# Order of the sums, the W_h product and the values in layer 3 of a graph network

## The chip, the cores and the metric

One core of one Trainium2 chip runs the whole program. The metric is device time in microseconds. Engines are TensorE (PE), VectorE (DVE), ScalarE (ACT), GpSimd (POOL) and SyncE (SP); each runs its own list of instructions, and semaphores tie them together.

## The reference

Four layers work on x (32 graphs of 512 nodes with 64 features) and one adjacency matrix; each adds its result to x. Layers 0 to 2 are a graph convolution, a two-step convolution and a graph attention. The change touches only layer 3, an attention network of 8 heads and an output layer of the same form:

```
def gat_layer(x, graph, W, b):
    h = x @ W
    s = jnp.einsum('bnd,bmd->bnm', h, h) * graph
    s = jnp.where(s == 0.0, NEG_INF, s)
    a = jax.nn.softmax(s, axis=2)
    return jnp.einsum('bnm,bmd->bnd', a, h) + b
heads = jax.vmap(lambda W, b: gat_layer(flow_x, graph, W, b))(Wh, bh)
...
x = jax.nn.leaky_relu(cat, negative_slope=0.01)
out = gat_layer(x, graph, W_out, b_out)
return jax.nn.leaky_relu(out, negative_slope=0.01)
```

## The kernel before

Layers 0 to 2 take the first 450 us or so and are not touched. Layer 3 works on units. A heads unit (class Heads) is two heads of one graph; an output unit (class Out) is the output layer of two graphs. There are 128 of the first and 16 of the second, 144 in all, mostly eight heads units to one output unit; the last eight units are all output units. A unit is a pair k = 0, 1 of attention matrices of 512 x 512, and is worked in four row blocks r of 128 rows (128 partitions x 2 x 512 columns).

One call of period(t) (line 737) issues work for several units in different stages: unit(lag) is the unit that is lag places behind. The engines' orders are written out by hand: what stands earlier in period(t) stands earlier in the queue of its engine, on all five engines. The stages of a unit, with the lag at which they are done:

- scores (L383): TensorE forms a row block's two score matrices in PSUM, each from 64 of the array's rows. Blocks 0 and 1 are made one period ahead (lag -1), blocks 2 and 3 at lag 0.
- maxima (L395): VectorE adds the mask, writes the negated scores to SBUF (p) and keeps each row's extreme. spread_out and spread_in (L402, L410): SyncE sends these to DRAM (top_row) and brings them back copied to all partitions (topb).
- shift (L416, L420), at lag 1: GpSimd subtracts topb from p, in the order of row blocks 0, 2, 1, 3. exps (L429): ScalarE exponentiates; for odd blocks into PSUM (e_ps), and join (L432) on VectorE adds the even block before it.
- totals (L450), at lag 2: TensorE multiplies with ones to sum over rows, into a PSUM tile tot_ps; ScalarE copies it (L456); two small transfers, one from SyncE's and one from ScalarE's queue, lay it out as parts (L461). recips (L467, L470): VectorE adds the parts and takes reciprocals; recips_out (L474) and, at lag 3, recips_in (L481) spread them by way of DRAM (recb).
- values (L438), at lag 2: TensorE multiplies the attention matrices with the features into av, the only tile of the pool ps_v. normalize (L487), at lag 3: VectorE multiplies av by recb, which frees av.
- y_pe (L568), y_act (L578) and y_dve (L586), at lag 4: the W_h product of heads units in PSUM, then the bias and the leaky relu into cat. L578 writes 0.01 (y + b); L586 reads y again and takes the maximum. An output unit does back (L670, L675) and back_dve (L678) in this place.
- product (L613): TensorE adds cat times W_out into gT_ps; the cat of a unit is needed in the period in which it is made or in the next.

PSUM is handed out by pools of tiles. ps_s has two tiles of two banks, taken in turn by score blocks and by the exponentials of odd blocks. ps_m has two tiles of one bank; tot_ps, the two y_ps, back_ps, gV_ps, hx_ps and the two g_ps take them in turn in the order in which they are issued, and each waits until its buffer's last reader is done.

At a period's end come smaller steps: the transposes hx_ps (L310) and gV_ps (L629), the products g_ps (L550), their copies on ScalarE (L562), and features (L509 to L528), which normalises a graph ahead of its use.

Of the kernel before, what the change touches and what calls it, by code (L numbers as in the profile page):

```python
# [22 lines left out]
def fast_form(  # L23
# [25 lines left out]
    nc = tc.nc  # L49
    B, N, F = x.shape  # L50
    C = N // P
# [643 lines left out]
    def any_zero():  # L695

        def across(src, rows, name):
            ps = ps_m.tile([P, P], F32, name=name, tag="m")
            n = src.shape[0]
            nc.tensor.transpose(ps[:rows, :n], src, ident[:n, :n])  # L700
            return ps[:rows, :n]

        own = tiny.tile([P, 1], F32, name="own")
        nc.vector.tensor_reduce(own, least, AX.X, OP.min)
        two = tiny.tile([1, 2], F32, name="two")
        nc.vector.tensor_reduce(two[:, 0:1], across(own, 1, "own_ps"), AX.X, OP.min)
        best = tiny.tile([B // 2, 2], F32, name="best")
        nc.vector.tensor_reduce(
            best,
            across(least_out, B // 2, "out_ps").rearrange("b (k f) -> b k f", k=2),  # L710
            AX.X, OP.max,
        )
        worst = tiny.tile([B // 2, 1], F32, name="worst")
        nc.vector.tensor_reduce(worst, best, AX.X, OP.min)
        nc.vector.tensor_reduce(
            two[:, 1:2], across(worst, 1, "worst_ps"), AX.X, OP.min
        )
        flag = tiny.tile([1, 1], F32, name="flag")
        nc.vector.tensor_reduce(flag, two, AX.X, OP.min)
        nc.vector.scalar_tensor_tensor(  # L720
            again, flag, 0.0, unsound, op0=OP.is_equal, op1=OP.max
        )
# [6 lines left out]
    def planned(units, products):  # L729

        class Nothing:
            def __getattr__(self, name):
                return lambda *args: None

        nothing = Nothing()

        def period(t):
            def unit(lag):
                return units[t - lag] if 0 <= t - lag < len(units) else nothing

            now, ahead = unit(0), unit(-1)
            for r in range(2, C):
                now.scores(r)
            unit(3).recips_in()
            unit(6).store()
            unit(4).bias()
            if t != 1:
                unit(1).shift(0, nc.gpsimd)
                unit(1).exps(0)
            unit(2).totals()  # L750
            unit(2).totals_out(1, nc.scalar)
            u, h = products.get(t - 1, (None, 0))
            if u and h == H - 1:
                u.keep_product()
            if t != 1:
                unit(1).shift(2, nc.gpsimd)
                unit(1).exps(2)
            for r in range(2, C):
                now.maxima(r)
            now.spread_out()  # L760
            unit(2).totals_out(0, nc.sync)
            now.spread_in()
            for r in range(2):
                ahead.scores(r)
            unit(4).y_pe()
            unit(4).y_act()
            unit(3).normalize()
            for r in range(2):
                ahead.maxima(r)
            if t == 1:  # L770
                for r in (0, 2, 1, 3):
                    unit(1).shift(r, nc.vector)
                    if r < 3:
                        unit(1).exps(r)
            unit(4).back()
            unit(4).y_dve()
            unit(4).back_dve()
            if t != 1:
                unit(1).shift(1, nc.gpsimd)
                unit(1).exps(1)  # L780
            for j in range(C):
                unit(2).values(j)
            u, h = products.get(t, (None, 0))
            if u:
                u.product(h)
            unit(2).recips()
            unit(2).recips_out()
            unit(1).join(1)
            if t != 1:
                unit(1).shift(3, nc.gpsimd)  # L790
            unit(1).exps(3)
            unit(5).back_pool()
            unit(-2).make_gs()
            unit(1).join(3)
            unit(-3).features(3)
            unit(-2).judge_product()
            unit(1).make_v()
            unit(-4).make_hx()
            unit(-2).make_g()
            for step in range(3):  # L800
                for lag, odd in ((step - 7, 0), (step - 11, 1)):
                    u = unit(lag)
                    if getattr(u, "i", None) == 0 and u.b % 2 == odd:
                        u.features(step)
            if t == len(units) + 1:
                any_zero()

        return period
# [1067 lines left out]
```

## Time and profile before

| | us |
|---|---|
| median of 3 runs (lowest to highest) | 2043.86 (2043.75 to 2046.07) |
| profiled execution, its time | 2045.32 |
| its span | 2043.5 |
| PE busy | 1980.7 (97%) |
| DVE busy | 1753.4 (86%) |
| POOL busy | 1445.8 (71%) |
| ACT busy | 1295.2 (63%) |
| PE busy between 560 and 1900 us | 1335.7 of 1340 |

The granted clock of TensorE is 0.989 over the span. A busy share is a mean over all four layers; in layer 3 alone TensorE has work in nearly every moment. A line of the timeline gives the start, the time until the end of the last instruction merged into it, the engine and the line of the kernel, and, in brackets, the idle time ahead of it and what released it. Matmuls overlap: the distance from one start to the next is a better measure than the length.

### The profile page before, as it was taken

The numbers are of one execution on the slowest core, as the hardware profiler recorded it, in microseconds if no ns is written. First come the engines' busy times: TensorE is split into PE (matmuls) and PEld (weight loads), VectorE is DVE, ScalarE is ACT, GpSimd is POOL, SyncE is SP. The second block draws the span as 40 slices with busy tenths as digits, with TensorE's granted clock in tenths as the row PEclk, the third lists the DMA queues.
The fourth block names the chain that finished last, engine by engine and source line by source line (L and its number), as shares of the span: only waits on it lengthen the run. The fifth ranks groups of instructions, "written<-read, shape, count | busy, mean of one in ns | idle before, by whom it ended". The sixth has DMA issues, their size and how long they took to land.

```text
span 2043.5 us, 32571 instructions
## 1 busy us (share of the span) xinstructions
PE 1980.7 (97%) x11038; PEld 811.0 (40%) x11038; DVE 1753.4 (86%) x4121; ACT 1295.2 (63%) x1960; POOL 1445.8 (71%) x834
## 2 busy tenths in 40 slices
PE   7999999997999999999999999999999999999995
PEld 4676676762333333333333333333333333333332
DVE  6699996768988899889898898888898898888984
ACT  3443443346677777777677777676676776766674
POOL 2000000006898989899999989898888988889996
PEclk9999999988999999999999999999999999999999
DMA  5000000002222323232332323333232323323233
GB/s 143 1 1 1 1 2 1 1 1 69 70 73 79 82 77 75 79 80 79 75 85 74 84 69 85 75 77 76 76 77 69 79 75 69 79 74 80 71 83 81
DMA packets 186464, 129.31 MB, mean 63 GB/s; under 512 B 125048, under 2 KB 130336, under 8 KB 186160
## 3 DMA queue, kind: packets, MB, share of 16 engines
q1 hardware_dynamic: 167056, 126.35, 23.9%
q10 hardware_dynamic: 18720, 0.59, 0.5%
q8 instruction: 89, 1.46, 0.3%
q14 instruction: 87, 0.71, 0.1%
q0 software_dynamic: 512, 0.20, 0.1%
HBM read 119.48 MB, written 5.37 MB: 61 GB/s over the span
## 4 chain that ended last, share of the span: by engine, by line
PE 57%; POOL 8%; DVE 4%; DMA 4%; ACT 2%; issue 2%; ACTq 0%; SPq 0%; POOLq 0%; DVEq 0%
PE s_ps L383 20%; PE av L438 19%; POOL p_att L416 6%; PE tot_ps L450 5%; PE y_ps L568 5%; PE gT_ps L613 4%; PE g_ps L550 3%; DMA topb<-top_row 2%; DVE p_att L395 2%; POOL p_att L420 2%; DVE p_att L432 1%; DMA top_row<-top 1%; PE hx_ps L310 1%; ACT e_ps L429 1%; DVE cat L586 1%
## 5 line engine op out<-in xcount | busy, mean ns | idle before, releaser
L416 POOL TENSOR_TENSOR p_att<-p_att,topb 128x1024 f32<-128x1024 f32 x429 | 1008.1, 2383 | 0.0
L395 DVE CUSTOM_DVE_ANT_0 p_att<-s_ps,flow_neg 128x512 f32<-128x512 f32 x1152 | 726.1, 686 | 91.2 <-PE s_ps L383 89.6
L383 PE MATMUL s_ps<-g,hx 64*128 64x512 f32 x2048 | 515.3, 613 | 16.6 <-DVE p_att L432 14.5
L420 POOL TENSOR_TENSOR p_att<-p_att,topb 128x512 f32<-128x512 f32 x286 | 360.5, 1282 | 170.5 <-DMA topb<-top_row 140.1
L429 ACT ACTIVATE p_att<-p_att 128x1024 f32<-128x1024 f32 x288 | 304.8, 1059 | 173.7 <-POOL p_att L420 91.1
L432 DVE TENSOR_TENSOR p_att<-e_ps,p_att 128x1024 f32<-128x1024 f32 x288 | 338.9, 1198 | 35.5 <-ACT e_ps L429 34.3
L429 ACT ACTIVATE e_ps<-p_att 128x1024 f32<-128x1024 f32 x288 | 293.1, 1029 | 88.1 <-POOL p_att L416 81.3
L383 PEld LDWEIGHTS s_ps<-g,hx 64*128 64x128 f32 x2048 | 174.8, 186 | 329.0 <-DVE top L395 173.8
L438 PE MATMUL av<-p_att,hd 128*64 128x512 f32 x1024 | 269.7, 605 | 0.0
L438 PE MATMUL av<-p_att,hn 128*64 128x512 f32 x1024 | 263.2, 592 | 0.0
L1090 POOL TENSOR_TENSOR x<-x,bias_b 128x512 f32<-128x512 f32 x16 | 20.3, 1274 | 280.3 <-DVE hn L863 280.3
L586 DVE SCALAR_TENSOR_TENSOR cat<-y_ps,bh,cat 128x512 f32<-128x512 f32 x256 | 180.1, 745 | 15.3 <-ACT cat L578 14.0
L562 ACT COPY g<-g_ps 128x512 f32<-128x512 f32 x128 | 131.8, 1138 | 81.1 <-PE g_ps L550 81.1
L578 ACT ACTIVATE cat<-y_ps,bh 128x512 f32<-128x512 f32 x256 | 161.4, 682 | 33.1 <-PE y_ps L568 32.2
L450 PE MATMUL tot_ps<-p_att,ones 128*32 128x512 f32 x1152 | 156.1, 607 | 4.0 <-DVE p_att L432 4.0
L568 PE MATMUL y_ps<-o_att,wh_sb 64*128 64x512 f32 x512 | 137.4, 594 | 0.0
L438 PEld LDWEIGHTS av<-p_att,hn 128*64 128x64 f32 x1024 | 73.7, 137 | 146.1 <-issue 146.1
L613 PE MATMUL gT_ps<-cat,wo_sb 128*64 128x512 f32 x512 | 131.6, 592 | 0.0
L438 PEld LDWEIGHTS av<-p_att,hd 128*64 128x64 f32 x1024 | 62.2, 136 | 165.4 <-issue 132.5
L1014 PE MATMUL acc<-v,s 64*128 64x65 f32 x2048 | 124.0, 280 | 0.7 <-DVE s L1000 0.4
L487 DVE TENSOR_TENSOR o_att<-av,recb 128x512 f32<-128x512 f32 x144 | 99.2, 689 | 29.4 <-DMA recb<-rec_row 26.8
L1014 PEld LDWEIGHTS acc<-v,s 64*128 64x128 f32 x2048 | 121.0, 194 | 5.9 <-DVE o L1030 1.2
(183 smaller groups left out, 2113.9 us busy)
## 6 DMA issues: line engine op xcount, KB each, us to landing
topb<-top_row SPq DMA_DIRECT2D x288, 256.0 KB
recb<-rec_row SPq DMA_DIRECT2D x288, 128.0 KB
out_dram<-y SPq DMA_DIRECT2D x32, 128.0 KB
x<-in_x_dram SPq DMA_DIRECT2D x3, 1024.0 KB
top_row<-top SPq DMA_DIRECT2D x144, 4.0 KB
parts<-tot SPq DMA_DIRECT2D x144, 4.0 KB
parts<-tot ACTq DMA_DIRECT2D x144, 4.0 KB
rec_row<-rec_flow SPq DMA_DIRECT2D x144, 4.0 KB
```

The costliest lines, as they stand in the source:

```text
L383: nc.tensor.matmul(ps[:, k], lhsT=x[halves(k), r * P : (r + 1) * P], rhs=g[halves(k), :], start=True, stop=True,)
L395: nc.vector.tensor_tensor_reduce(out=self.p[r][:, k], in0=ps[:, k], in1=flow_neg[:, r], scale=-1.0, scalar=BIG, op0=OP.add, op1=OP.min, ac ...
L416: engine.tensor_tensor(self.p[r], self.p[r], self.topb, OP.subtract)
L420: engine.tensor_tensor(p, p, self.topb[:, k], OP.subtract)
L429: nc.scalar.activation(to, self.p[r], AF.Exp, scale=-1.0)
L432: nc.vector.tensor_tensor(self.p[r], self.joined, self.p[r - 1], OP.add)
L438: nc.tensor.matmul(self.av[halves(k), :], lhsT=self.v(k, j) if j % 2 else self.less_next(k, j), rhs=self.p[j][:, k], start=(j == 0), stop= ...
L450: nc.tensor.matmul(ps[q : q + 32, :], lhsT=ones, rhs=self.p[2 * e + 1][:, k], start=True, stop=True,)
L568: nc.tensor.matmul(ps, lhsT=wh_sb[halves(k), 2 * self.i + k, :], rhs=self.o[halves(k), :], start=True, stop=True,)
L586: nc.vector.scalar_tensor_tensor(self.cat[:, k], self.y[k], bh[:, h : h + 1], self.cat[:, k], op0=OP.add, op1=OP.max,)
L613: nc.tensor.matmul(self.gps[halves(k), :], lhsT=wo_sb[:, h, :], rhs=Heads.cat.pop((self.b + k, h)), start=(h == 0), stop=(h == H - 1),)
L1014: nc.tensor.matmul(self.acc[k][:, r], lhsT=self.s[b // 2][halves(k), b % 2, r * P : (r + 1) * P], rhs=self.v[halves(k), b], start=(b == 0) ...
```

## The change

Only the order of the calls in period(t) changes. On TensorE the W_h product comes between score blocks 2, 3 and the next unit's blocks 0, 1, the sums come behind all four blocks, and the W_out product comes ahead of the values. On ScalarE the W_h product's bias follows the exponential of row block 2 and the copy of the sums follows it. On VectorE L586 comes straight after normalize and ahead of the next unit's maxima, and the reciprocals come between the two additions. On SyncE the transfer of the parts goes behind both topb transfers.

```
             if t != 1:
                 unit(1).shift(0, nc.gpsimd)
                 unit(1).exps(0)
-            unit(2).totals()
-            unit(2).totals_out(1, nc.scalar)
             u, h = products.get(t - 1, (None, 0))
             if u and h == H - 1:
                 u.keep_product()
             if t != 1:
                 unit(1).shift(2, nc.gpsimd)
                 unit(1).exps(2)
+            unit(4).y_pe()
+            unit(4).back()
+            unit(4).y_act()
             for r in range(2, C):
                 now.maxima(r)
             now.spread_out()
-            unit(2).totals_out(0, nc.sync)
             now.spread_in()
             for r in range(2):
                 ahead.scores(r)
-            unit(4).y_pe()
-            unit(4).y_act()
             unit(3).normalize()
+            unit(4).y_dve()
+            unit(4).back_dve()
+            unit(2).totals()
+            for e, queue in enumerate((nc.sync, nc.scalar)):
+                unit(2).totals_out(e, queue)
             for r in range(2):
                 ahead.maxima(r)
...
-            unit(4).back()
-            unit(4).y_dve()
-            unit(4).back_dve()
             if t != 1:
                 unit(1).shift(1, nc.gpsimd)
                 unit(1).exps(1)
-            for j in range(C):
-                unit(2).values(j)
             u, h = products.get(t, (None, 0))
             if u:
                 u.product(h)
+            for j in range(C):
+                unit(2).values(j)
+            unit(1).join(1)
             unit(2).recips()
             unit(2).recips_out()
-            unit(1).join(1)
```

More of the change, by code (lines that the diff above doesn't have):

```diff
@@ L749, in period @@
                 unit(1).exps(0)
-            unit(2).totals()
-            unit(2).totals_out(1, nc.scalar)
             u, h = products.get(t - 1, (None, 0))
@@ L757, in period @@
                 unit(1).exps(2)
+            unit(4).y_pe()
+            unit(4).back()
+            unit(4).y_act()
             for r in range(2, C):
@@ L760, in period @@
             now.spread_out()
-            unit(2).totals_out(0, nc.sync)
             now.spread_in()
@@ L764, in period @@
                 ahead.scores(r)
-            unit(4).y_pe()
-            unit(4).y_act()
             unit(3).normalize()
+            unit(4).y_dve()
+            unit(4).back_dve()
+            unit(2).totals()
+            for e, queue in enumerate((nc.sync, nc.scalar)):
+                unit(2).totals_out(e, queue)
             for r in range(2):
@@ L774, in period @@
                         unit(1).exps(r)
-            unit(4).back()
-            unit(4).y_dve()
-            unit(4).back_dve()
             if t != 1:
@@ L780, in period @@
                 unit(1).exps(1)
-            for j in range(C):
-                unit(2).values(j)
             u, h = products.get(t, (None, 0))
@@ L785, in period @@
                 u.product(h)
+            for j in range(C):
+                unit(2).values(j)
+            unit(1).join(1)
             unit(2).recips()
             unit(2).recips_out()
-            unit(1).join(1)
             if t != 1:
```

## The prediction

> **What bounds the kernel now.** I read the page's shares first, then the costliest groups, then the waits, then the timeline of single periods. A period is one call of period(t); S is the start of its first score block (score blocks 2 and 3 of unit t).
>
> ```profile
> PE 1980.7 (97%) x11038; PEld 811.0 (40%) x11038; DVE 1753.4 (86%) x4121; ACT 1295.2 (63%) x1960; POOL 1445.8 (71%) x834
> ...
> L416 POOL TENSOR_TENSOR p_att<-p_att,topb 128x1024 f32<-128x1024 f32 x429 | 1008.1, 2383 | 0.0
> ...
> L420 POOL TENSOR_TENSOR p_att<-p_att,topb 128x512 f32<-128x512 f32 x286 | 360.5, 1282 | 170.5 <-DMA topb<-top_row 140.1
> ```
>
> TensorE is 97% busy; in the middle of layer 3 (560 to 1900 us) it is busy 1335.7 of 1340 us. So any wait put ahead of a TensorE instruction costs its whole length. GpSimd subtracts the row minima (shift): two halves and three whole tiles, 2 x 1.28 + 3 x 2.38 = 9.7 us, and what it waits for is the topb transfer. The timeline of TensorE over one ordinary period:
>
> ```profile
> 1218.96 1.99 PE L383 MATMUL s_ps<-g,hx 64*128 64x512 f32 x8
> 1220.88 1.06 PE L450 MATMUL tot_ps<-p_att,ones 128*32 128x512 f32 x8
> 1221.88 1.99 PE L383 MATMUL s_ps<-g,hx 64*128 64x512 f32 x8
> 1223.70 1.02 PE L568 MATMUL y_ps<-o_att,wh_sb 64*128 64x512 f32 x4
> 1224.65 1.08 PE L438 MATMUL av<-p_att,gD 128*64 128x512 f32 x4
> ```
>
> The starts follow one another with hardly a hole: two score blocks 1.9, sums 1.0, two score blocks 1.8, W_h product (y) 0.95, values 3.5, W_out product 0.9, and what ends a period (g, hx or gV) 0.6 to 1.0. Nine periods (eight of heads, one of the output layer) take 1307.18 - 1210.16 = 97.0 us from sums to sums. The one with the output unit's transposes lasts 1251.05 - 1240.82 = 10.2, so one of heads lasts (97.0 - 10.2) / 8 = 10.85. The other engines in that period:
>
> ```profile
> 1218.22 2.50 POOL L420 TENSOR_TENSOR p_att<-p_att,topb 128x512 f32<-128x512 f32 x2 [1.80 <-DMA topb<-top_row]
> ...
> 1220.68 7.03 POOL L416 TENSOR_TENSOR p_att<-p_att,topb 128x1024 f32<-128x1024 f32 x3
> ...
> 1222.59 0.69 DVE L487 TENSOR_TENSOR o_att<-av,recb 128x512 f32<-128x512 f32 x1
> ...
> 1223.19 1.06 ACT L429 ACTIVATE p_att<-p_att 128x1024 f32<-128x1024 f32 x1 [0.59 <-POOL p_att L416]
> ...
> 1224.75 1.27 ACT L578 ACTIVATE cat<-y_ps,bh 128x512 f32<-128x512 f32 x2 [0.51 <-PE y_ps L568]
> ```
>
> The exponential of row block 2 starts at S + 4.2, when GpSimd's second shift is done; y is then copied and biased by ScalarE, and VectorE's maximum follows (L586, 0.75 each). None of this holds TensorE today: sums run at S + 1.9, before y exists.
>
> **The Trainium skill.** "PSUM — Partial Sum Buffer", section "Engine vs sequencer instructions", says that ScalarE, VectorE and GpSimdE queues are strict FIFO and that matmuls start and complete in program order. The traced order agrees: everything on an engine stands in the order of period(t). "DMA: Bandwidth & Descriptors", section "Anatomy of one DMA", gives about 2.0 us of fixed cost, mostly completion. Here SyncE waited 237.6 us in 144 cases for rec_row, 1.65 each, 1.97 with the 0.32 of issue. "Perfetto Trace Analysis", section "Optimization Strategy", says consistent bubbles on the engine that should be saturated can mean too few PSUM buffers; the trace before shows next to none at the sums (the L450 matmuls idled 4.0 us in the whole run).
>
> **The change part by part.**
>
> *TensorE order.* New: scores 2, 3; y; scores 0, 1 of the next unit; sums; W_out product; values. Scores and y have the same tile shape (64 x 128), so two shape changes around the sums go, and one (sums to W_out product) comes. From the start differences: scores to sums to scores cost 0.1 + 0.14 above 1.72 and 0.86, y to values 0.09. The new period with no wait is 5 x 0.86 + 0.1 = 4.4 before the sums, then 0.95 + 0.88 + 3.49 + 0.62 (mean of the endings) + 0.1 = 6.0: 10.4 to 10.5. That alone is 0.25 to 0.35 less than now.
>
> *A wait that comes in.* ps_m has two buffers. Before, the sums took them ahead of y0 and y1; now y0, y1 and then the sums take them in turn, so the sums need y0's buffer. Its last reader is the first L586 on VectorE. That stands behind L578 on ScalarE, which in the new order stands behind the exponential of row block 2, which waits for GpSimd's second shift. Measured from S at today's spacing, over ten periods from 1208 to 1315 us: the first shift starts 9.81 after the S of the period before; two halves and one whole tile, 4.81 from start to start, end at 14.62; +0.12 to the exponential, +0.96 until the next ScalarE instruction starts, 0.68 for L578, 0.03, 0.72 for L586, 0.1 to TensorE: the sums start at 17.23, which is S + 6.4 in today's 10.8. TensorE is there at S + 4.45. The stall is 2.0; the W_out product (which needs the second L586, 0.65 later) is then covered by the sums' 0.95, and values, the endings and the next period's scores all wait behind.
>
> *Feedback.* The shift follows scores of the period before, so a longer period brings it relatively earlier. Two periods = 17.23 + 6.0 = 23.2: 11.6 each. (Today's spacing would give 12.4; half the excess remains.)
>
> *The reciprocals' round.* Before, nothing led from normalize (L487) back to the sums. Now VectorE does L487 before L586 in the same queue, so a round of one period closes: sums to copy 1.13 and 0.59; the parts transfer, at most 3.2 by the rows (3.2 to 4.7 passed with no wait), but hidden, for the reduction stands behind the addition of row block 1, which needs its exponential after the copy and its 0.5 of DMA issue: 4.55 after the sums; reduction and reciprocal 0.35; rec_row 0.1 and 1.4 to 1.97 (1.4 where topb has landed, as it will have here); recb 3.6 (issue to L487 where it waited); L487 0.62, L586 0.72, 0.1: 11.45 to 12.0. It is about as long as the other round.
>
> *ScalarE in front of it.* In three of eight head periods (ScalarE's timeline: activations at 1232.07, 1253.09 and 1274.50 right after g's copies) the two copies (to S + 2.3) and the features' activations (1.06 to 1.26) come ahead of both exponentials: 2.3 + 1.1 + 2 x 0.96 + 0.68 + 0.75 + 0.1 = 6.75 for the sums, and 12.7 with 6.0 behind; since the next period can give some back, I take 12.3. Eight head periods: (5 x 11.6 + 3 x 12.3) / 8 = 11.86, 1.0 over today's 10.85. Some is lent back, so 0.95.
>
> *Queues.* SyncE issues the parts transfer after topb instead of before it: topb was waiting for top_row there anyway (131 us over 127 cases), so nothing is won; the parts come behind 512 KB of topb, hidden as above. ScalarE's parts issue moves with the copy. The output unit's transposes, one period in nine, hold no y buffer: no change. Join 1 ahead of the reciprocals costs nothing where the parts have landed, and it delays rec_row by 1.2, already counted. Layers 0 to 2 (to 450 us) are untouched.
>
> *Sum.* 128 head units x 0.95 = +122 us on the profiled span of 2043.5 (2045.3 with what lies around it; the median of the runs is 2043.9): 2165 us.
>
> **Rivals.** (a) The mean transfers are slower: rec_row at up to 4.0 and top_row at 3.0 as in their tails, with recb now later and so in front of top_row. The round is 12.2, +1.3 x 128 = 166: 2210. For it: both rounds are close, and the later of two counts every time. Against: topb no longer collides with rec_row. (b) Slow periods lend to fast ones and the output period resets the chain: nine periods are four pairs of 23.2 less shared endings and one of 10.2, some 102, +0.55 a period: 2115. (c) Other side: y's reader is in time and only the saved shape changes remain: -0.25 x 136 = -34, 2010. It would take L586 at S + 4.4, 1.9 us earlier than the table, so that GpSimd or ScalarE would have to run ahead of today; the 1.8 us that GpSimd waited for topb in the fenced line speak against slack there. (d) The buffers are not taken in turn and no wait arises; then (c) again or no change.
>
> **How the numbers follow.** Main case 0.5; (a) 0.22; (b) 0.17; (c) and (d) faster 0.08; unchanged 0.03. Slower 0.89. 0.2%, 4 us, is what a measurement can tell from no change. The range 2090 to 2225 leaves out the faster cases and the far end of (a); the main case alone is 2140 to 2190.
>
> **What would show it.** TensorE idle just before L450, some 1 to 2 us in head periods, released by VectorE's cat (L586); TensorE near 91%; the waits for topb on GpSimd grow; L487 waits for recb in most periods; L578 no longer waits for TensorE. Wrong if L450 has no idle time before it, if the stall stands at another line (values on L487, y on g's copy), or if head periods stay near 10.8.

## The result and the profile after

The changed kernel takes 2246.3 us in the median (2240.5 to 2250.5) against 2043.8 before: a ratio of 1.099, interval 1.095 to 1.102. It is slower, as forecast, but by 202.5 us where 121 were forecast, and it lies outside the range of 2090 to 2225.

The page after, shares and the groups that the prediction spoke of (in a group: busy time and mean of one, then the engine's idle time just before and what ended it):

```profile
PE 2020.9 (90%) x11038; PEld 846.0 (38%) x11038; DVE 1771.0 (79%) x4121; ACT 1290.2 (58%) x1960; POOL 1442.8 (64%) x834
...
L420 POOL TENSOR_TENSOR p_att<-p_att,topb 128x512 f32<-128x512 f32 x286 | 361.1, 1282 | 368.1 <-DMA topb<-top_row 321.7
...
L450 PE MATMUL tot_ps<-p_att,ones 128*32 128x512 f32 x1152 | 158.3, 622 | 145.5 <-DVE cat L586 144.4
...
L586 DVE SCALAR_TENSOR_TENSOR cat<-y_ps,bh,cat 128x512 f32<-128x512 f32 x256 | 179.7, 743 | 54.0 <-ACT cat L578 53.8
...
L487 DVE TENSOR_TENSOR o_att<-av,recb 128x512 f32<-128x512 f32 x144 | 99.4, 690 | 100.2 <-DMA recb<-rec_row 96.6
```

TensorE's busy time grows by 40 us and that of the others by less than 18. This growth is not more work, since the ends of matmuls are modelled: from the first to the last of the values' sixteen starts 3.04 us pass in the mean, 3.06 before. So the clock is not the cause either, though the one granted was 0.984 in this run and 0.989 before. The time is a new stall: TensorE stands ahead of the sums (L450) until VectorE's L586, where it hardly stood before. GpSimd's wait for topb grows from 140 to 322 us and L487's for recb from 27 to 97, both as announced. The chain that ended last, before the change 57% TensorE, is now this:

```profile
PE 26%; DMA 18%; ACT 14%; DVE 12%; issue 4%; POOL 2%; SPq 1%; ACTq 1%; DVEq 0%; POOLq 0%
```

One period of the timeline (start, us, engine, line; in brackets the idle time and its releaser):

```profile
1220.79 0.69 DVE L487 TENSOR_TENSOR o_att<-av,recb 128x512 f32<-128x512 f32 x1 [0.83 <-DMA recb<-rec_row]
1221.21 1.26 ACT L578 ACTIVATE cat<-y_ps,bh 128x512 f32<-128x512 f32 x2
...
1221.93 1.41 DVE L586 SCALAR_TENSOR_TENSOR cat<-y_ps,bh,cat 128x512 f32<-128x512 f32 x2 [0.45 <-ACT cat L578]
...
1222.74 1.07 PE L450 MATMUL tot_ps<-p_att,ones 128*32 128x512 f32 x8 [1.24 <-DVE cat L586]
1223.73 1.08 PE L613 MATMUL gT_ps<-cat,wo_sb 128*64 128x512 f32 x4
```

Here both late things meet at L586: recb held L487, and L578 then held L586 for 0.45 more. VectorE's waits for the two between 560 and 1900 us (us, times, longest; there are 110 periods):

```profile
DVE o_att L487 <- DMA recb<-rec_row: 66.6, 77, 2.2
DVE cat L586 <- ACT cat L578: 46.4, 41, 2.4
```

Taken period by period in this stretch of the trace, in 102 periods of heads only recb held VectorE ahead of the first L586 in 50, only L578 in 21, both in turn in 20, and neither in 11. The parts of a period, as means of the distances between starts in the timelines (560 to 1900 us, every unit): before, 1.96 from the first score block to the sums, 3.81 to the values, 5.02 to the next period's scores, 10.8 in all. After, 6.11, 1.95 and 4.19: 12.25. The period is 1.45 longer; 195.2 us of added span are 135 such periods.

### The profile page after: what moved, and what is told of

Read it like the earlier page. It is cut to its first block, busy times and chain, and to the rows that moved or that the text cites. A ratio compares the mean times of both kernels' runs of the same rounds, so it can differ in the third digit from the quotient of the medians.

```text
span 2238.7 us, 32504 instructions
## 1 busy us (share of the span) xinstructions
PE 2020.9 (90%) x11038; PEld 846.0 (38%) x11038; DVE 1771.0 (79%) x4121; ACT 1290.2 (58%) x1960; POOL 1442.8 (64%) x834
## 4 chain that ended last, share of the span: by engine, by line
PE 26%; DMA 18%; ACT 14%; DVE 12%; issue 4%; POOL 2%; SPq 1%; ACTq 1%; DVEq 0%; POOLq 0%
PE av L438 11%; DMA recb<-rec_row 8%; PE tot_ps L450 7%; DMA rec_row<-rec_flow 4%; ACT g L562 4%; DVE cat L586 4%; DMA parts<-tot 4%; PE gT_ps L613 3%; DVE p_att L395 3%; ACT p_att L429 3%; PE g_ps L550 2%; PE s_ps L383 2%; ACT e_ps L429 2%; DVE p_att L432 2%; DMA top_row<-top 2%
## 5 line engine op out<-in xcount | busy, mean ns | idle before, releaser
L395 DVE CUSTOM_DVE_ANT_0 p_att<-s_ps,flow_neg 128x512 f32<-128x512 f32 x1152 | 726.2, 685 | 113.5 <-PE s_ps L383 112.9
L383 PE MATMUL s_ps<-g,hx 64*128 64x512 f32 x2048 | 552.7, 610 | 21.8 <-DVE p_att L432 15.3
L432 DVE TENSOR_TENSOR p_att<-e_ps,p_att 128x1024 f32<-128x1024 f32 x288 | 345.2, 1199 | 59.4 <-ACT e_ps L429 59.2
L429 ACT ACTIVATE p_att<-p_att 128x1024 f32<-128x1024 f32 x288 | 297.8, 1054 | 91.1 <-POOL p_att L416 68.4
L429 ACT ACTIVATE e_ps<-p_att 128x1024 f32<-128x1024 f32 x288 | 285.2, 1020 | 99.0 <-DVE top L395 75.9
L383 PEld LDWEIGHTS s_ps<-g,hx 64*128 64x128 f32 x2048 | 205.5, 186 | 288.1 <-DVE top L395 114.3
L450 PE MATMUL tot_ps<-p_att,ones 128*32 128x512 f32 x1152 | 158.3, 622 | 145.5 <-DVE cat L586 144.4
L456 ACT COPY tot<-tot_ps 128x512 f32<-128x512 f32 x144 | 84.3, 585 | 265.2 <-PE tot_ps L450 265.2
L586 DVE SCALAR_TENSOR_TENSOR cat<-y_ps,bh,cat 128x512 f32<-128x512 f32 x256 | 179.7, 743 | 54.0 <-ACT cat L578 53.8
L487 DVE TENSOR_TENSOR o_att<-av,recb 128x512 f32<-128x512 f32 x144 | 99.4, 690 | 100.2 <-DMA recb<-rec_row 96.6
L568 PE MATMUL y_ps<-o_att,wh_sb 64*128 64x512 f32 x512 | 168.7, 599 | 0.0
L578 ACT ACTIVATE cat<-y_ps,bh 128x512 f32<-128x512 f32 x256 | 159.8, 676 | 4.5 <-PE y_ps L568 4.5
L613 PE MATMUL gT_ps<-cat,wo_sb 128*64 128x512 f32 x512 | 145.1, 647 | 0.0
L438 PEld LDWEIGHTS av<-p_att,hd 128*64 128x64 f32 x1024 | 74.0, 139 | 155.9 <-issue 144.6
```

Source lines behind the costliest of these rows:

```text
L383: nc.tensor.matmul(ps[:, k], lhsT=x[halves(k), r * P : (r + 1) * P], rhs=g[halves(k), :], start=True, stop=True,)
L395: nc.vector.tensor_tensor_reduce(out=self.p[r][:, k], in0=ps[:, k], in1=flow_neg[:, r], scale=-1.0, scalar=BIG, op0=OP.add, op1=OP.min, ac ...
L429: nc.scalar.activation(to, self.p[r], AF.Exp, scale=-1.0)
L432: nc.vector.tensor_tensor(self.p[r], self.joined, self.p[r - 1], OP.add)
L438: nc.tensor.matmul(self.av[halves(k), :], lhsT=self.v(k, j) if j % 2 else self.less_next(k, j), rhs=self.p[j][:, k], start=(j == 0), stop= ...
L450: nc.tensor.matmul(ps[q : q + 32, :], lhsT=ones, rhs=self.p[2 * e + 1][:, k], start=True, stop=True,)
```

## The experiments

The theory at the start: two rounds of dependencies meet at L586, the reciprocals' (sums, parts, rec_row, recb, L487, L586, sums) and GpSimd's (scores, topb, shift, exponential, L578, L586, sums). The rival: only one of them matters. For each kernel the mean period is given (distance from sums to sums between 560 and 1900 us, all units; where the stretch is cut moves it by up to 0.02); it is 10.80 before and 12.25 after.

**One round opened, then the other, then both.**

First, L578 goes ahead of the exponential on ScalarE:

```
-            if t != 1:
-                unit(1).shift(2, nc.gpsimd)
-                unit(1).exps(2)
             unit(4).y_pe()
             unit(4).back()
             unit(4).y_act()
+            if t != 1:
+                unit(1).shift(2, nc.gpsimd)
+                unit(1).exps(2)
```

> The changed kernel, with the W_h product's bias (L578) ahead of the exponential of row block 2 on ScalarE. Theory: two rounds meet at L586, and the reciprocals' round (sums, parts, rec_row, recb, normalize, L586, sums) of one period is the longer. Then only the lateness of L578 goes, 0.47 us between normalize and L586 in the mean of the changed kernel: 128 x 0.45 = 58 us off 2246, some 2190 us, with recb still waited for. Rival: GpSimd's shift by way of L578 sets the period and recb is only waited for because there is time: then this edit takes the stall away, 2010 to 2060 us.

Measured: 2203.5 us, ratio 1.078 (1.076 to 1.080), period 11.94. Only 43 us go, and VectorE still waits for recb (75.2 us in 76 cases between 560 and 1900), while L586 still waits for L578 in 24 cases (17.4 us). So the reciprocals' round holds the time nearly by itself.

Second, L586 goes ahead of normalize on VectorE:

```
-            unit(3).normalize()
             unit(4).y_dve()
             unit(4).back_dve()
+            unit(3).normalize()
```

> The changed kernel, with L586 (and the output unit's maximum) ahead of normalize on VectorE, so that nothing leads from recb to the sums. Theory: the period falls to that of GpSimd's round, 11.6 to 11.9 us for a heads unit against 12.35 now: 2150 to 2180 us, TensorE still idle ahead of L450, now behind L578. Rival (GpSimd's round alone set the period already): 2230 to 2250 us, as now.

Measured: 2194.3 us, ratio 1.073 (1.072 to 1.075), period 11.90. 52 us go, somewhat fewer than I expected. Among the waits of this kernel's VectorE between 560 and 1900 us hardly any is for recb any more; L586 waits for L578 instead:

```profile
DVE cat L586 <- ACT cat L578: 138.8, 92, 3.0
DVE p_att L395 <- PE s_ps L383: 61.3, 83, 2.4
DVE rec_flow L467 <- DMA parts<-tot: 35.0, 47, 1.8
DVE p_att L432 <- ACT e_ps L429: 6.1, 18, 0.7
...
DVE o_att L487 <- DMA recb<-rec_row: 1.8, 3, 0.9
```

The same round can be opened without touching any order, by taking away what makes L487 wait. This kernel multiplies by a tile that is ready and so leaves out the division by the sums:

```
-            nc.vector.tensor_tensor(self.o, self.av, self.recb, OP.mult)
+            nc.vector.tensor_tensor(self.o, self.av, urow, OP.mult)
```

> The changed kernel, where normalize multiplies by a tile that has lain ready since layer 2 (the node scales) instead of recb, so the division by the sums of the softmax is left out; all transfers are still issued, and L487 is as long as before and still ahead of L586. Theory: the reciprocals' round is open, GpSimd's round stays: 2170 to 2200 us, as with L586 ahead of normalize. Rival A (the round of the reciprocals alone made the time): below 2120 us. Rival B (recb was only waited for because there was time): 2235 to 2255 us.

Measured: 2196.6 us, ratio 1.073 (1.071 to 1.075), period 11.96; L586 waits for L578 for 83.6 us in 74 cases, and L487 for nothing. Two different edits, one on the queue and one on the transfer, give the same time. So GpSimd's and ScalarE's round is also a bound by itself, and nearly as long.

Third, both queue edits together:

> Both edits together: L578 ahead of the exponential, L586 ahead of normalize; TensorE's order is that of the changed kernel. Theory: neither round leads to the sums any more, the stall is at most what g's copies leave on ScalarE: 2000 to 2060 us, near the kernel before. Rival: the later sums make the reciprocals late all the same, or the buffer of y0 is late by TensorE's own order: over 2100 us.

Measured: 2110.0 us, ratio 1.032 (1.030 to 1.034), period 11.25. One edit gives 43, the other 52, both 136: as with two bounds of nearly one length, of which either holds what the other lets go. It misses my 2000 to 2060 and falls to the rival (over 2100): some 65 us of the loss belong to neither round. TensorE still stands 24.1 us ahead of the sums, in 41 cases between 560 and 1900.

**What is left without the rounds.** The next kernel adds to both edits that L578 stands ahead of both exponentials and of the copy of gT:

```
+            unit(4).y_pe()
+            unit(4).back()
+            unit(4).y_act()
             if t != 1:
                 unit(1).shift(0, nc.gpsimd)
                 unit(1).exps(0)
             u, h = products.get(t - 1, (None, 0))
...
-            unit(4).y_pe()
-            unit(4).back()
-            unit(4).y_act()
```

> As both edits together (L578 ahead of the exponential of block 2, L586 ahead of normalize, 2110 us), but L578 ahead of both exponentials and of the copy of gT on ScalarE. Theory: what was left of the stall at L450 (24 us between 560 and 1900) came from ScalarE's own work in front of L578 and shrinks by half or more, the rest of the gap to the kernel before is TensorE's order (scores to sums at least 4.82 us, no gain over the old order): 2085 to 2102 us. Rival: the first exponential, now later, delays the chain to the additions and takes it back: 2110 us or more.

Measured: 2093.2 us, ratio 1.024 (1.022 to 1.026), period 11.10. TensorE's waits between 560 and 1900 us no longer name the sums:

```profile
PE s_ps L383 <- DVE p_att L432: 14.5, 30, 1.3
PE gT_ps L613 <- ACT gT L621: 3.5, 8, 0.6
PE av L438 <- DVE o_att L487: 2.2, 3, 1.3
```

So the new order of TensorE, with no such stall at the sums, is still 0.30 longer per period than the old one. Its distance from scores to sums is 5.03 in the mean and never below 4.82. The chain that ended last in the kernel with both edits shows why, in order of time:

```profile
1229.39 1.08 PE s_ps L383 x4
1230.48 0.03 issue
1230.50 0.69 DVE p_att L395
...
1231.20 0.60 DVE p_att L395
...
1231.81 0.60 DVE p_att L395
...
1232.42 0.60 DVE p_att L395
...
1233.09 1.13 PE s_ps L383 x4
1234.22 1.00 PE tot_ps L450 x8
```

The next unit's second score block needs the buffer that VectorE reads last among four L395, so it starts 3.7 us after the period's start. Until then the new order gives TensorE four steps of 0.86 (two score blocks, the W_h product, the next unit's first block); the old order had the sums there too, and its second block started at 3.92. So VectorE sets the 4.82, where I had put TensorE's own 4.4. The list of waits does not name this hole: each block is shown with a modelled end 1.08 to 1.13 after its start, though the next can start 0.86 after it, and a hole as short as this is counted as busy. After a period that ends with g, the second y also waits for g's second copy: there the distance is 5.16 in the mean, otherwise 4.92.

**The sums alone.** In the kernel before, the sums move behind the next unit's two score blocks, with the copy and the parts; nothing else moves:

```
-            unit(2).totals()
-            unit(2).totals_out(1, nc.scalar)
...
-            unit(2).totals_out(0, nc.sync)
...
             for r in range(2):
                 ahead.scores(r)
+            unit(2).totals()
+            unit(2).totals_out(0, nc.sync)
+            unit(2).totals_out(1, nc.scalar)
             unit(4).y_pe()
```

> The kernel before, with only the sums (and their copy and the transfers of the parts) moved behind the next unit's two score blocks; the W_h product stays behind them, so the sums take their buffer ahead of y0 and wait for no L586. Theory: no stall at L450; recb comes about 0.5 us late for normalize, which holds VectorE, not TensorE: 2040 to 2085 us. Rival (late sums are what costs, through the reciprocals and not through the buffer): over 2150 us.

Measured: 2305.5 us, ratio 1.127 (1.125 to 1.129), period 12.64: far outside what I expected, and slower than the whole change. The number falls to the rival (over 2150), but its cause, the reciprocals, is not what the trace shows: between 560 and 1900 us L487 waits for recb only 5.5 us, in 11 cases. The timeline:

```profile
1223.07 2.26 PE L383 MATMUL s_ps<-g,hx 64*128 64x512 f32 x8 [0.65 <-DVE top L395]
...
1225.25 1.07 PE L450 MATMUL tot_ps<-p_att,ones 128*32 128x512 f32 x8
...
1226.25 1.90 PE L568 MATMUL y_ps<-o_att,wh_sb 64*128 64x512 f32 x4
1226.39 0.59 ACT L456 COPY tot<-tot_ps 128x512 f32<-128x512 f32 x1 [1.83 <-PE tot_ps L450]
...
1227.02 0.29 PEld L568 LDWEIGHTS y_ps<-o_att,wh_sb 64*128 64x128 f32 x2 [0.48 <-ACT tot L456]
...
1228.28 1.41 DVE L586 SCALAR_TENSOR_TENSOR cat<-y_ps,bh,cat 128x512 f32<-128x512 f32 x2 [1.10 <-ACT cat L578]
```

Two things that I had left out. The pool of two buffers ties in the other direction as well: with the sums next to the W_h product, the second y needs the buffer of the sums, and the pair of y takes 1.84 in the mean, from its start to that of the next tile, where it took 1.01. And the next unit's first block now waits 0.65 for VectorE, because the sums no longer fill the time before it: y starts 5.81 after the period's start, where it started at 4.79. These two, 0.83 and 1.02, are the whole of the 1.84 by which the period is longer. So this run doesn't tell the buffer from the place, as it was meant to; it shows that the old order had the two score blocks between the sums and y, which hid the sums' copy.

The hole ahead of the next unit's block was then measured alone, by moving one block ahead of the sums in the kernel before:

```
+            ahead.scores(0)
             unit(2).totals()
...
-            for r in range(2):
-                ahead.scores(r)
+            ahead.scores(1)
```

> The kernel before, with only one of the next unit's two score blocks moved ahead of the sums on TensorE: scores 2, 3, next 0, sums, next 1, W_h product. No buffer is taken in another order and the sums come one block later. Theory: next block 0 needs VectorE's maxima of block 2, which end at S + 2.4, so TensorE stands some 0.5 us that the sums used to fill: 144 x 0.5 = 72, 2095 to 2130 us. Rival: VectorE has slack and the sums' place among the blocks costs nothing, 2040 to 2055 us.

Measured: 2147.7 us, ratio 1.050 (1.048 to 1.052), period 11.56. TensorE waits for VectorE's maxima ahead of a score block:

```profile
PE s_ps L383 <- DVE top L395: 85.6, 141, 1.1
```

That is 0.6 in 141 of 144 units, as reckoned; with 102 us the loss is larger than these waits. The starts show the rest: the next unit's second block begins 4.65 after the period's start, where it began at 3.92, and this 0.73 is nearly all of the 0.76 by which the period is longer. The wait is counted from the modelled end of the block before and so falls short of the hole.

**The buffer.** The sums take the values' buffer in place of y0's; all orders stay those of the changed kernel:

```
-            ps = ps_m.tile([P, N], F32, name="tot_ps", tag="m")
+            ps = ps_v.tile([P, N], F32, name="tot_ps", tag="av")
...
-                self.av = ps_v.tile([P, N], F32, name="av")
+                self.av = ps_v.tile([P, N], F32, name="av", tag="av")
```

> The changed kernel with the sums in the values' PSUM buffer instead of the one of y0; all orders as in the changed kernel. Theory: the wait for y0's buffer is what ties the sums to L586; now they wait for normalize (L487), the last reader of the values, so recb still leads to them, but L586 and L578 no longer do, except where ScalarE's copy of the sums stands behind L578 and the values wait for that copy: the reciprocals' round is shorter by some 1.2 us, 2100 to 2165 us. Rival: the stall comes with the late place of the sums and not with the buffer: 2230 us or more.

Measured: 2191.0 us, ratio 1.071 (1.069 to 1.073), period 11.83. The sums' releaser changes to the last reader of the other buffer, as it must if the buffer is the tie:

```profile
PE tot_ps L450 <- DVE o_att L487: 50.5, 61, 2.6
```

The time falls by 55 us, not by the 81 to 146 that I expected: L487 waits for recb all the same (91.0 us in 87 cases). With L578 ahead of the exponential as well:

> The sums in the values' buffer, and L578 ahead of the exponential of row block 2. Theory: what was left through ScalarE's copy goes too, only normalize's wait for recb is in front of the sums: 2075 to 2115 us. Rival: no better than the buffer alone (within 10 us of it), because recb sets the period by itself.

Measured: 2165.3 us, ratio 1.059 (1.057 to 1.061), period 11.63. Here the reciprocals' round no longer passes through L586. Its pieces are: sums to copy 1.21, to the issue of the parts 0.75, to the reduction 3.12, to rec_row 0.43, to recb's issue 1.52, to L487 3.62, to the next sums 0.97; 11.62 in all. Pieces that lead from one sums to the next add up to the period whatever bounds it; that this round does so shows in its waits, of L487 for recb in 88 cases (84.1 us) and of the sums for L487 in 57 (48.4 us). The time lies 50 us above what I expected, and that of the kernel with the buffer alone 26 above: I had put this round too short.

**Two parts of the change undone in the changed kernel.** The reciprocals back ahead of both additions, and the W_out product back behind the values:

```
+            unit(2).recips()
+            unit(2).recips_out()
             unit(1).join(1)
-            unit(2).recips()
-            unit(2).recips_out()
```

> The changed kernel with the reciprocals back ahead of both additions on VectorE. Theory: the reciprocals' round sets the period in most heads units, and in it the reduction (L467) starts 2.95 us after the parts are issued, of which part is the addition of row block 1 in front; without it some 0.3 us of each round go: 2195 to 2220 us. Rival: the place of the reciprocals doesn't bear on the end, 2235 to 2255 us.

Measured: 2249.7 us, ratio 1.101 (1.098 to 1.104): no change to the kernel after. I had expected 25 us or more; the rival's value came. The trace shows that something did move: between 560 and 1900 us VectorE now stands 176.2 us for the parts, ahead of both additions (17.2 in the kernel after), and most of what TensorE wins at the sums (76.6 us of waiting against 116.6) it loses at the score blocks, which wait 37.9 us for the additions instead of 4.7.

```
-            u, h = products.get(t, (None, 0))
-            if u:
-                u.product(h)
             for j in range(C):
                 unit(2).values(j)
+            u, h = products.get(t, (None, 0))
+            if u:
+                u.product(h)
```

> The changed kernel with the W_out product back behind the values. Theory: its place neither costs nor saves, since L586 for the second head is over before the sums are: 2235 to 2255 us. Rival: it waits for cat in front of the values, and its old place gives 20 us or more back: below 2226 us.

Measured: 2242.9 us, ratio 1.096 (1.094 to 1.098): none either, as expected.

## Why the prediction was wrong

The sign, the place and the wait were right. The sum was too small, because it gave nothing to the meeting of the two rounds and put each of them somewhat too short. TensorE's new order, taken for a gain, is a loss; in the changed kernel the rounds are longer than that, and it shows only where they are opened.

*A wait that comes in* holds. L450's idle time, its releaser L586, the growth at topb and recb and TensorE at 90% are what it named. Where the buffer is changed, the releaser changes.

*TensorE order* failed. It put the period without a wait at 10.4 to 10.5, 0.25 to 0.35 less than before. (Against its own 10.85 for a unit of heads that would be 0.35 to 0.45 less.) Measured is 11.10, 0.30 more. I had added TensorE's blocks and left out that the next unit's score blocks need VectorE's four L395 of this period; the sums, a longer filler, had stood there. This also ends the rival (c): even without that stall at the sums the order is 48 us slower.

*Feedback* and *ScalarE in front of it* were too short. Their 11.86 for a heads unit is (8 x 11.86 + 10.2) / 9 = 11.68 over all units; the two kernels with the other round open measured 11.90 and 11.96. (The terms of the case with g's copies add up to 6.85, not 6.75; the 12.3 taken for it does not rest on that.) The entry of topb was right (3.77 + 2.12 + 3.72 = 9.6 from scores to first shift, forecast 9.81); the excess is behind it, with L578, for which VectorE waits 84 to 139 us in these kernels, and in TensorE's part from sums to scores, 6.1 where I had 6.0.

*The reciprocals' round* was given as 11.45 to 12.0 for a heads unit, 11.3 to 11.8 over all, and then set beside the other as "about as long". With L578 nearly out of the way it measured 11.94. The terms after the change: sums to reduction 1.17 + 0.70 + 2.96 = 4.8 (forecast 4.55), rec_row 1.55, recb 3.69, from L487 to L586 1.10 (forecast 0.62, since L578 is late too), from L586 to the sums 0.80.

*Sum* is the step that failed. It took the 1.0 of GpSimd's round alone, made it 0.95 because "some is lent back", and added nothing for the other round, found to be "about as long". But both lead to L586, and it has to wait for the later of the two in each period: in the changed kernel that was L578 in 41 periods of heads and recb in 50. Alone they give 11.90 to 11.96, together 12.25. In us: 149 to 158 above the kernel before with one round, 202.5 with both, 65 with neither and 48 with ScalarE's remainder gone too. The forecast of 0.95 x 8 / 9 = 0.84 per unit stands against a measured 1.45. Of the 0.61 that is missing, 0.26 to 0.32 is the round of GpSimd and ScalarE put too short (10.80 + 0.84 = 11.64 forecast, 11.90 and 11.96 measured), and 0.3 is the second round.

*Queues* holds: the place of the reciprocals and of the W_out product moved nothing that could be measured in the whole time; with the reciprocals first, one stall was exchanged for another.

Rival (a) came nearest in time, but not by its mechanism: no mean transfer became slower. Only what it gave in its favour, that the later of two close rounds counts every time, is what the runs bear out. From the issue of rec_row to that of recb the mean fell from 2.02 to 1.55, from recb's issue to L487 from 3.86 to 3.69, from top_row's to topb's from 2.17 to 2.12. Rival (b), slow periods lending to fast ones, is refuted by the mean period itself. No kernel here beats the one before.

What stays open: how much of the 0.3 by which the two rounds together exceed either is chance (the later of two that vary) and how much is one making the other later. In the changed kernel the period is 13.1 in the mean where L578 came last and 11.9 where only recb held; no run separates the two.

## What to carry to other kernels

When a product moves in a saturated engine's order, write down for each pool of buffers who now takes a buffer from whom, and follow that reader back: a round that closes within one period is a bound of its own. With two such bounds take the later one in each period, which comes to more than either of them alone, and expect that repairing one of them alone gives little. And ask what stood in the place that the moved work left: it may have been filling another engine's time.

## What was not expected of the hardware

The prediction says that matmuls start in program order and that the trace agrees. In the records of TensorE there are exceptions, and the measurement decides. In the period shown above, the second y waits for the buffer of g's copy, and the first matmul of the next score block, which works on the other 64 rows of the array, starts ahead of the last one of y:

```profile
1218.92 0.59 PE L383 MATMUL s_ps<-g,hx 64*128 64x512 f32 x1
1219.19 0.59 PE L568 MATMUL y_ps<-o_att,wh_sb 64*128 64x512 f32 x1
```

Between 560 and 1900 us this happened 49 times after the change (44 with y, 5 with g) and 6 times before (with g), by one matmul each time. Nothing in the argument rests on it.

The small transfer rec_row (4 KB) took less time in the changed kernel although the kernel is slower, as the prediction had allowed for: 1.55 us in the mean from its issue to the issue that waits for it, 1.39 at best, against 2.02 before. Before, it was issued between the issue of topb and the first shift in 116 of 124 periods, with 2.08 in the mean, and 1.41 in the other 8; after the change this was so in 1 of 109 periods. The parts, issued behind the two topb transfers on the same queue, were reduced 2.2 us later at the earliest and 2.96 in the mean. VectorE waited for them in 28 of 110 periods only; with the reciprocals ahead of both additions it waited in 102, and there they took 2.90. How much of this comes from the 512 KB ahead of them, no run shows.
